# A transposed scratch image with x outermost, a residual moved in one transfer per step, and gathered pixels kept in channel order

## The chip, the cores and the metric

The kernel runs on one core of a Trainium2 chip. A core has TensorE (PE, matrix multiplies), VectorE (DVE), ScalarE (ACT), GpSimd (POOL) and SyncE (SP); each works through its own instructions in order, and they wait for one another by semaphores. Data lies in device memory (DRAM), in the on-chip memory of 128 partitions (SBUF) or in TensorE's output memory (PSUM). Transfers are done by 16 DMA engines, which all queues share; in this kernel nearly all DMAs are issued by GpSimd, a smaller part by SyncE. The metric is the device time of one execution in microseconds (us); lower is better.

## The reference

There are two layers over `x` of shape (8, 32, 128, 128), that is 8 images of 32 channels. `_gn` is a normalisation over groups of two channels. The first layer finds, for every pixel, the 8 of 25 neighbouring offsets with the smallest patch distance, gathers the 8 shifted pixels in each of the 32 channels, and works on the 256 gathered channels; channel `c*8 + k` holds channel `c` at the k-th best offset.

```python
def layer0(x, dct_w, w1, w2, w3, w4, w5, w6, inv_dct_w, agg_w):
    xb = patch_match_stack(x)              # (8, 256, 128, 128), channel c*8 + k
    dct = conv(xb, dct_w, groups=32)       # mixes the 8 pixels of one channel c
    h = relu(conv(conv(xb, w1), w2, groups=256, pad=1))   # 1x1, then 3x3 per channel
    h = relu(conv(conv(h, w3), w4, groups=256, pad=1))
    wiener = sigmoid(conv(conv(h, w5), w6, groups=256, pad=1))
    filt = conv(wiener * dct, inv_dct_w, groups=32)
    return conv(filt, agg_w)               # back to 32 channels

x = x + layer0(_gn(x), ...)
x = x + conv5x5(_gn(x), kernel)            # the same 5x5 kernel for each channel
```

## The kernel before

**Preparing an image.** `prep` loads an image with four groups of 32 rows over four groups of 32 partitions (`xn`, L81), normalises it (L384) and starts two things. `sources` (L399) makes a transposed copy for the gather: eight times, TensorE transposes four rows of each group into PSUM (L407), ScalarE copies the result to `xs` (L409), and GpSimd stores it, one DMA per row of the four, into the DRAM tile `xl` (L411). `xl` is laid out as (y, x, channel). Then 30 DMAs from DRAM to DRAM (L424), and two more for the borders (L429), spread it into `xtd`, in which the pixels that one gather tile needs lie together. `squares` and `costs` compute the patch distances: VectorE subtracts (L444), ScalarE squares (L452), TensorE sums over channels into `pd` (L459), ScalarE copies to `sm` (L470), GpSimd stores to `sq` (L474) and reads back into `dsum` (L492, L499); VectorE sums over the patch into `v` (L508 and on) and takes the 8 best of 25 (L536, L537). `places` turns them into bytes and stores them in the DRAM tile `idxd` (L573).

**Gathering.** A unit is four rows of half an image's width. `gather_load` brings the pixels `xt` (L591) and the indices `ib` (L602, one of three buffers, so it waits for the selection three units back). `gather_select` makes one-hot rows `sel` from `ib` on ScalarE (L616, L617). `gather_pixels` multiplies them with the pixels on TensorE (L631), copies the result to `xb` on ScalarE (L638) and, after every fourth unit, stores `xb`, eight rows of all 256 gathered channels, to the DRAM tile `xbd` with one DMA of 1 MB (L640). In `xb` partition `32 j + c` and index `g` hold channel `c` at offset `k = 2 j + g`; `xbd` has the same order, (128, 2, y, x).

**Filtering.** A step is eight rows. Each image has 17 steps, the last for the rows that the three 3x3 convolutions lag behind. For each of three stages the 1x1 convolution runs on TensorE (L670, L694) and the 3x3 one half on VectorE (L724) and half on TensorE (L750), which first needs rows moved between partitions, the transfers `t<-t` on SyncE's queue (L706, L708). `final_load` fetches the residual `xr` (L780, four DMAs, one per quarter of the partitions) and the gathered pixels `xf` (L790, eight DMAs, because the 256 channels must lie on the partitions in the order that `ldct` needs, while `xbd` keeps them by offset). `final_dct` applies `dct_w` on TensorE into `pc` (L809) and multiplies it in on VectorE (L817); `final_add` applies the aggregation into `pa` (L830), adds the residual (L838), takes statistics (L839) and stores the sum to the DRAM tile `x1d` (L843, four DMAs). The first and last step of an image have fewer than eight rows and use a layout of their own; the other 15 are `whole`. `layer1` reads `x1d` back (`xy`, `xm`), applies the 5x5 kernel on TensorE (L923) and stores to the output (L937).

**Order.** The order on TensorE, VectorE and ScalarE is written out by hand: the main loop runs over 17 x 8 steps (and two more to drain), in each over the stages 3, 2, 1 and 0 (0 is the final part), and works on one gather unit per stage. The preparation of the next image is cut into pieces that stand in queues, from which the loop takes VectorE work against a budget, and the rest as soon as it is due. GpSimd's instructions keep an order of their own, in which a DMA waits until its data and its buffer are ready and everything behind it waits too. `final_load` of a step is issued at the end of the loop's turn, one step ahead of its use. `mixes` (L300) builds `ldct` and the combined weights `lagg` once at the start, `weights` the others.

Of the kernel before, what the change touches and what calls it, by code (L numbers as in the profile page):

```python
# [8 lines left out]
F32 = mybir.dt.float32  # L9
# [7 lines left out]
P = 128  # L17
C, K, H, W = 32, 8, 128, 128
CK = C * K
NO = 25  # L20
R = 8
NS = H // R
TW = 11
# [13 lines left out]
C_M32 = C_G2 + 32  # L37
# [7 lines left out]
def bm3d_conv_preact(  # L45
# [16 lines left out]
    nc = tc.nc  # L62
# [237 lines left out]
    def mixes():  # L300

        dq = work.tile([P, 2, K], F32, name="dq", tag="dq", bufs=1)
        src = dct_w.rearrange("(m h c i) k a b -> m h k c (i a b)", m=2, h=2, i=K)
        for k in range(K):
            for m in range(2):
                for h in range(2):
                    p = 64 * h + 32 * (k % 2) + 8 * (k // 2)
                    nc.sync.dma_start(dq[p : p + 8, m], src[m, (h + m + 1) % 2, k])
        m8 = work.tile([P, 8], F32, name="m8", tag="m16", bufs=1)
        yield "D", 1.0, 10  # L310
        nc.vector.tensor_reduce(
            m8,
            cst[:, C_M32 : C_M32 + C].rearrange("p (a c) -> p c a", c=8),
            axis=mybir.AxisListType.X,
            op=ALU.add,
        )
# [82 lines left out]
    def sources(b, xn):  # L399


        xl = dram.tile([H, W, C], F32, name=f"xl_{b}", tag="xl")
        for r in range(0, 32, 4):
            yield "P", 0
            pt = ps_x.tile([P, 4, P], F32, name=f"px_{b}_{r}", tag="x")
            for q in range(4):
                nc.tensor.transpose(pt[:, q], xn[:, 3 + r + q, 2 : 2 + W], ident)  # L407
            xs = work.tile([P, 4, P], F32, name=f"xs_{b}_{r}", tag="ct")
            nc.scalar.copy(xs, pt)  # L409
            for q in range(4):  # L410
                nc.gpsimd.dma_start(  # L411
                    xl.rearrange("(g r) x c -> r x g c", g=4)[r + q],
                    xs[:, q].rearrange("p (g c) -> p g c", c=C),
                )
        xt = xtd[b] = dram.tile([H, QW, NT, C], F32, name=f"xtd_{b}", tag="xtd")
        for j in range(QW):
            for f in range(2):
                ta, tz = f * (NT // 2), (f + 1) * (NT // 2)
                if j < 2 and f == 0:
                    ta += 1  # L420
                if HW * f + TW * (NT // 2 - 1) + j - 2 >= W:
                    tz -= 1
                xa = HW * f + TW * (ta - f * (NT // 2)) + j - 2
                nc.gpsimd.dma_start(  # L424
                    xt[:, j, ta:tz], xl[:, xa : xa + TW * (tz - ta - 1) + 1 : TW]
                )
        jz = W + 2 - HW - TW * (NT // 2 - 1)
        for ja, jz, t, at in ((0, 2, 0, 0), (jz, QW, NT - 1, W - 1)):
            nc.gpsimd.dma_start(  # L429
                xt[:, ja:jz, t], xl[:, at : at + 1].to_broadcast([H, jz - ja, C])  # L430
            )

    def squares(b, i, pd, xn, aa, sq, idx):
# [186 lines left out]
    def gather_pixels(b, s4, f):  # L620
# [16 lines left out]
                )  # L637
        nc.scalar.copy(xb[:, :, 4 * h : 4 * h + 4, HW * f : HW * (f + 1)], pg)  # L638
        if h == 1 and f == 1:
            nc.gpsimd.dma_start(xbd[b][:, :, R * n : R * (n + 1)], xb)  # L640

# [88 lines left out]
    def depthwise_t(i, b, n):  # L732
# [33 lines left out]
        rows_before_t(i, b, n)  # L766
        accs[i, b, n][0] = acc

    def final_load(b, n):
        j0, j1 = (3, R) if n == 0 else (0, R if n < NS else 3)  # L770
        ya, yz = R * n - 3 + j0, R * n - 3 + j1

        whole = j1 - j0 == R
        nr, nw = (2, W) if whole else (j1 - j0, C)
        xr = work.tile([P, 2 * W], F32, name=f"xr_{b}_{n}", tag="xr")
        xr = xr[:, : nr * nw].rearrange("p (r w) -> p r w", w=nw)
        for j in range(4):
            ra = ya + 2 * j if whole else ya
            xa = 0 if whole else C * j
            nc.gpsimd.dma_start(  # L780
                xr[C * j : C * (j + 1)], x[b, :, ra : ra + nr, xa : xa + nw]
            )

        xf = xbp.tile([P, 2, R, W], F32, name=f"xf_{b}_{n}", tag="xf", bufs=1)
        src = xbd[b].rearrange("(j m h c) g y x -> g m h j c y x", j=4, m=2, h=2)
        for m in range(2):
            for h in range(2):
                for g in range(2):
                    p = 64 * h + C * g
                    nc.gpsimd.dma_start(  # L790
                        xf[p : p + C, m, j0:j1], src[g, m, (h + m + 1) % 2, :, :, ya:yz]
                    )
        return xr, xf, j0, j1

    def final_dct(b, n, acc, xf, j0, j1):
# [23 lines left out]
    def final_add(b, n, acc, xr, j0, j1):  # L819
# [17 lines left out]
        yield  # L837
        nc.vector.tensor_add(xr, xr, pa)  # L838
        nc.vector.bn_stats(stats[b][:, n], xr)  # L839
        for j in range(4):  # L840
            ra = ya + 2 * j if whole else ya
            xa = 0 if whole else C * j
            nc.gpsimd.dma_start(  # L843
                x1d[b][:, ra : ra + nr, xa : xa + nw], xr[C * j : C * (j + 1)]
            )

    def layer1(b):
# [186 lines left out]
    with tc.manual_schedule(engines=ORDERED):  # L1034
        push(prep(0))
        push(weights())
        push(mixes())
        xbd[0] = dram.tile([P, 2, H, W], F32, name="xbd_0", tag="xbd")
        for i in range(3):
            nc.gpsimd.memset(tb[i][0:64, :, 0], 0.0)  # L1040
        for u in range(7):
# [12 lines left out]
        for s in range(len(steps) + 2):  # L1054
            if s < len(steps):
# [5 lines left out]
                    push(prep(b + 1))  # L1061
                if n == NS - 1 and b + 1 < NB:
                    until(lambda: b + 1 in ready, 4.0)
                    xbd[b + 1] = dram.tile([P, 2, H, W], F32, name=f"xbd_{b+1}", tag="xbd")
            for i in (3, 2, 1, 0):
                si = s - (i - 1 if i else 2)
                live = 0 <= si < len(steps)
# [109 lines left out]
```

## Time and profile before

| What | Before |
|---|---|
| Median of 3 runs | 6640.18 us |
| Lowest and highest run | 6636.07 and 6641.82 us |
| The profiled execution: time, span | 6645.45 us, 6643.7 us |
| Mean granted clock of TensorE | 0.978 |
| Busy: PE, DVE, ACT, POOL | 6238.3, 5862.9, 5054.4, 3079.3 us |
| POOL instructions | 5015 |
| DMA | 770751 packets, 886.20 MB, mean 133 GB/s |

The span runs from the first to the last instruction. Busy time leaves out register, branch and semaphore instructions; on POOL a `DMA_DIRECT2D` row is the time that GpSimd takes to issue one transfer, not the transfer. "<-" after an idle time names what ended the wait; where several things are waited for, it is the one that came last by the profile's records, and it can be wrong. "The chain that ended last" is found by walking back from the last instruction, each time to what released it. Tiles are named without their numbers: `xf<-xbd` is a transfer from `xbd` to `xf`.

### The profile page before, as it was taken

The numbers are of one execution on the slowest core, as the hardware profiler recorded it, in microseconds if no ns is written. First come the engines' busy times: TensorE is split into PE (matmuls) and PEld (weight loads), VectorE is DVE, ScalarE is ACT, GpSimd is POOL, SyncE is SP. The second block draws the span as 40 slices with busy tenths as digits, with TensorE's granted clock in tenths as the row PEclk, the third lists the DMA queues.
The fourth block names the chain that finished last, engine by engine and source line by source line (L and its number), as shares of the span: only waits on it lengthen the run. The fifth ranks groups of instructions, "written<-read, shape, count | busy, mean of one in ns | idle before, by whom it ended". The sixth has DMA issues, their size and how long they took to land.

```text
span 6643.7 us, 234197 instructions
## 1 busy us (share of the span) xinstructions
PE 6238.3 (94%) x102306; PEld 3236.5 (49%) x102306; DVE 5862.9 (88%) x8828; ACT 5054.4 (76%) x6698; POOL 3079.3 (46%) x5015
## 2 busy tenths in 40 slices
PE   5898899999999999999999999999999999999997
PEld 1444455544555545544555544554445544454553
DVE  7889988999889998898989998899888999887786
ACT  5787778777787777877778877887769777687772
POOL 8354346444464343643446444464435543344334
PEclk8899999999999999999999999999999999999998
DMA  4555555656555564655646656465555655556553
GB/s 85 126 138 130 131 131 130 148 134 140 131 143 136 130 147 118 149 134 133 144 121 147 147 126 149 120 154 136 130 137 132 148 136 130 125 141 145 137 133 82
DMA packets 770751, 886.20 MB, mean 133 GB/s; under 512 B 248880, under 2 KB 614000, under 8 KB 769728
## 3 DMA queue, kind: packets, MB, share of 16 engines
q0 software_dynamic: 383648, 611.87, 36.9%
q1 hardware_dynamic: 383568, 258.11, 17.6%
q8 instruction: 805, 13.19, 0.9%
q10 hardware_dynamic: 2512, 1.25, 0.1%
q14 instruction: 218, 1.79, 0.1%
HBM read 420.60 MB, written 216.49 MB: 96 GB/s over the span
## 4 chain that ended last, share of the span: by engine, by line
PE 43%; DVE 29%; DMA 9%; ACT 8%; POOL 6%; issue 4%; SPq 0%; ACTq 0%; DVEq 0%; POOLq 0%
DVE acc L724 20%; PE pw L750 14%; PE pv L670 11%; PE p L694 9%; PE pg L631 3%; DMA t<-t 3%; POOL xtd L424 2%; DVE df L444 2%; DVE idx L537 2%; PE pc L809 2%; ACT sel L616 2%; ACT df L452 2%; DMA xf<-xbd 2%; DVE acc L817 1%; PE p L923 1%
## 5 line engine op out<-in xcount | busy, mean ns | idle before, releaser
L724 DVE SCALAR_TENSOR_TENSOR acc<-tv,dwv,acc 128x1024 f32<-128x1024 f32 (+3 forms) x3264 | 4032.3, 1237 | 240.8 <-ACT acc L721 136.8
L750 PE MATMUL pw<-t,dwd 96*32 96x254 f32 (+7 forms) x31680 | 2124.6, 420 | 51.0 <-DMA t<-t 38.4
L750 PEld LDWEIGHTS pw<-t,dwd 96*32 96x32 f32 (+1 forms) x31680 | 1088.4, 110 | 874.5 <-issue 411.2
L616 ACT ACTIVATE sel<-ib,nplace 128x1024 f32<-128x1024 uint8 x1024 | 1172.1, 1145 | 37.4 <-DMA ib<-idxd 37.4
L617 ACT ACTIVATE sel<-sel 128x1024 f32<-128x1024 f32 x1024 | 1085.7, 1060 | 32.5
L694 PE MATMUL p<-acc,lw 128*32 128x256 f32 x16768 | 1002.9, 383 | 24.7 <-ACT tv L678 23.3
L670 PE MATMUL pv<-acc,lw 128*32 128x512 f32 x8448 | 956.2, 590 | 48.7 <-DVE acc L817 43.4
L602 POOL DMA_DIRECT2D ib<-idxd x512 | 292.5, 571 | 1241.8 <-ACT sel L616 1176.2
L790 POOL DMA_DIRECT2D xf<-xbd x1088 | 651.9, 631 | 316.1 <-PE pc L809 180.1
L694 PEld LDWEIGHTS p<-acc,lw 128*32 128x32 f32 x16768 | 579.2, 111 | 437.1 <-issue 79.4
L452 ACT ACTIVATE df<-df 128x786 f32<-128x786 f32 (+2 forms) x576 | 468.6, 861 | 340.5 <-DVE df L444 337.8
L631 PE MATMUL pg<-sel,xt 120*32 120x88 f32 (+1 forms) x24576 | 616.1, 244 | 63.6 <-ACT sel L617 50.7
L631 PEld LDWEIGHTS pg<-sel,xt 120*32 120x32 f32 x24576 | 556.8, 110 | 235.0 <-ACT sel L617 70.1
L678 ACT COPY tv<-pv 128x512 f32<-128x512 f32 (+2 forms) x784 | 437.1, 579 | 305.0 <-PE pv L670 293.0
L444 DVE TENSOR_TENSOR df<-xn 128x786 f32<-128x786 f32 (+2 forms) x576 | 531.6, 973 | 81.2 <-PE pd L459 80.2
L728 ACT ACTIVATE acc<-acc 128x1024 f32<-128x1024 f32 (+3 forms) x408 | 417.3, 1023 | 241.6 <-DVE acc L724 241.3
L763 ACT ACTIVATE acc<-pw 128x512 f32<-128x512 f32 (+2 forms) x808 | 438.5, 573 | 182.7 <-PE pw L750 182.0
L670 PEld LDWEIGHTS pv<-acc,lw 128*32 128x32 f32 x8448 | 286.0, 111 | 534.1 <-issue 428.7
L701 ACT COPY t<-p 128x512 f32<-128x512 f32 x800 | 424.4, 571 | 118.0 <-PE p L694 118.0
L721 ACT ACTIVATE acc<-tv,dwv 128x1024 f32<-128x1024 f32 (+3 forms) x408 | 454.9, 1115 | 33.9 <-PE pa L830 20.6
L670 PE MATMUL pv<-xb,lw 128*32 128x512 f32 x4096 | 473.5, 596 | 0.0
L694 PE MATMUL p<-xb,lw 128*32 128x256 f32 x8192 | 468.5, 379 | 1.0 <-DVE xy L935 0.9
(155 smaller groups left out, 5932.9 us busy)
## 6 DMA issues: line engine op xcount, KB each, us to landing
ib<-idxd POOLq DMA_DIRECT2D x512, 256.0 KB, 4.1
xbd<-xb POOLq DMA_DIRECT2D x128, 1024.0 KB, 5.9
xf<-xbd POOLq DMA_DIRECT2D x960, 128.0 KB, 7.1
t<-t SPq DMA_DIRECT2D x792, 128.0 KB
t<-t SPq DMA_DIRECT2D x384, 256.0 KB
tv<-tv SPq DMA_DIRECT2D x384, 130.0 KB
xt<-xtd POOLq DMA_DIRECT2D x240, 180.0 KB, 3.7
xtd<-xl POOLq DMA_DIRECT2D x192, 96.0 KB, 3.5
```

The source lines that it names most:

```text
L444: nc.vector.tensor_sub(df[:, :, ca:cz], xn[:, r0 : r0 + SR, ca:cz], xn[:, r0 + dy : r0 + dy + SR, ca + dx : cz + dx],)
L452: nc.scalar.activation(df[:, :, ca:cz], df[:, :, ca:cz], AF.Square)
L616: nc.scalar.activation(sel, ib, AF.Square, bias=nplace)
L617: nc.scalar.activation(sel, sel, AF.Relu, scale=-1.0, bias=1.0)
L631: nc.tensor.matmul(pg[C * j : C * (j + 1), :, :, xa:xz], xt[: 8 * QW, f * (NT // 2) + t], sels[j // 2][: 8 * QW, j % 2 * 2 : j % 2 * 2 + 2 ...
L670: nc.tensor.matmul(ps[C * j : C * (j + 1), :hr], lhsT[:, g, P + C * j : P + C * (j + 1)], src(g)[:, h : h + hr], start=g == 0, stop=g == 1,)
L694: nc.tensor.matmul(ps[C * r : C * (r + 1), e, :nb], lhsT[:, g, s], rows[:, r : r + 4 * nb - 3 : 4], start=g == 0, stop=g == 1,)
L721: nc.scalar.activation(acc, rows, AF.Copy, scale=tap)
L724: nc.vector.scalar_tensor_tensor(acc, rows, tap, acc, op0=ALU.mult, op1=ALU.add)
L750: nc.tensor.matmul(pt[u][C * j : C * (j + 1), ka:kz, :nb, xa:xz], dwd[0:hi, i - 1, u, j, dx + 1], t[0:hi, j, ka:kz, :nb, xa + dx : xz + dx ...
L763: nc.scalar.activation(rows[:, u : u + 2 * nh[u] - 1 : 2, :nb], pt[u][:, : nh[u], :nb], funcs[i - 1])
L790: nc.gpsimd.dma_start(xf[p : p + C, m, j0:j1], src[g, m, (h + m + 1) % 2, :, :, ya:yz])
```

## The change

- `xl` becomes (x, y, channel). The copy to `xs` puts the four rows of a group next to each other, so that a piece of four rows by 32 channels (512 B) is contiguous on both sides, and one DMA replaces four. The reads into `xtd` take the same pixels with the new strides.
- `xbd` becomes (256, y, x) in the reference's channel order `c*8 + k`. Its store takes four DMAs, one per `j`, in place of one.
- `xf` is read in whole blocks of channels with three DMAs in place of eight. The halves of the first block are still swapped.
- The residual's load and the store of its sum take one DMA in place of four in the 15 whole steps.
- `mixes` lays the weights out to suit: the rows of `dq` go to partition `64 h + 8 c + k` in place of `64 h + 32 (k % 2) + 8 (k / 2) + c`, with the same number of loads, and the mask `m8` is taken from other columns of the constants.

```diff
@@ mixes
-        src = dct_w.rearrange("(m h c i) k a b -> m h k c (i a b)", m=2, h=2, i=K)
-        for k in range(K):
+        src = dct_w.rearrange("(m h c i) k a b -> m h c k (i a b)", m=2, h=2, i=K)
+        for c in range(8):
             for m in range(2):
                 for h in range(2):
-                    p = 64 * h + 32 * (k % 2) + 8 * (k // 2)
-                    nc.sync.dma_start(dq[p : p + 8, m], src[m, (h + m + 1) % 2, k])
+                    p = 64 * h + K * c
+                    nc.sync.dma_start(dq[p : p + K, m], src[m, (h + m + 1) % 2, c])
...
-            cst[:, C_M32 : C_M32 + C].rearrange("p (a c) -> p c a", c=8),
+            cst[:, C_M16 : C_M16 + 16].rearrange("p (a c) -> p c a", c=8),
@@ sources
-        xl = dram.tile([H, W, C], F32, name=f"xl_{b}", tag="xl")
+        xl = dram.tile([W, H, C], F32, name=f"xl_{b}", tag="xl")
...
-            nc.scalar.copy(xs, pt)
-            for q in range(4):
-                nc.gpsimd.dma_start(
-                    xl.rearrange("(g r) x c -> r x g c", g=4)[r + q],
-                    xs[:, q].rearrange("p (g c) -> p g c", c=C),
-                )
+            nc.scalar.copy(
+                xs.rearrange("p g (q c) -> p q g c", c=C),
+                pt.rearrange("p q (g c) -> p q g c", c=C),
+            )
+            nc.gpsimd.dma_start(
+                xl.rearrange("x (g r) c -> x g (r c)", g=4)[:, :, C * r : C * (r + 4)], xs
+            )
...
                 nc.gpsimd.dma_start(
-                    xt[:, j, ta:tz], xl[:, xa : xa + TW * (tz - ta - 1) + 1 : TW]
+                    xt[:, j, ta:tz],
+                    xl[xa : xa + TW * (tz - ta - 1) + 1 : TW].rearrange("x y c -> y x c"),
                 )
@@ gather_pixels
-            nc.gpsimd.dma_start(xbd[b][:, :, R * n : R * (n + 1)], xb)
+            for j in range(4):
+                nc.gpsimd.dma_start(
+                    xbd[b].rearrange("(c j g) y x -> j c g y x", j=4, g=2)[
+                        j, :, :, R * n : R * (n + 1)
+                    ],
+                    xb[C * j : C * (j + 1)],
+                )
@@ final_load (by_rows is image[:, ya : ya + R] as "c (j r) w -> j c (r w)")
-        for j in range(4):
-            ra = ya + 2 * j if whole else ya
-            xa = 0 if whole else C * j
+        if whole:
+            nc.gpsimd.dma_start(by_channel(xr), by_rows(x[b], ya))
+        for j in range(0 if whole else 4):
             nc.gpsimd.dma_start(
-                xr[C * j : C * (j + 1)], x[b, :, ra : ra + nr, xa : xa + nw]
+                xr[C * j : C * (j + 1)], x[b, :, ya : ya + nr, C * j : C * (j + 1)]
             )
...
-        src = xbd[b].rearrange("(j m h c) g y x -> g m h j c y x", j=4, m=2, h=2)
-        for m in range(2):
-            for h in range(2):
-                for g in range(2):
-                    p = 64 * h + C * g
-                    nc.gpsimd.dma_start(
-                        xf[p : p + C, m, j0:j1], src[g, m, (h + m + 1) % 2, :, :, ya:yz]
-                    )
+        for m, to, at, size in ((0, 0, 64, 64), (0, 64, 0, 64), (1, 0, P, P)):
+            nc.gpsimd.dma_start(xf[to : to + size, m, j0:j1], xbd[b][at : at + size, ya:yz])
@@ final_add
-        for j in range(4):
-            ra = ya + 2 * j if whole else ya
-            xa = 0 if whole else C * j
+        if whole:
+            nc.gpsimd.dma_start(by_rows(x1d[b], ya), by_channel(xr))
+        for j in range(0 if whole else 4):
             nc.gpsimd.dma_start(
-                x1d[b][:, ra : ra + nr, xa : xa + nw], xr[C * j : C * (j + 1)]
+                x1d[b][:, ya : ya + nr, C * j : C * (j + 1)], xr[C * j : C * (j + 1)]
             )
```

More of the change, by code (lines that the diff above doesn't have):

```diff
@@ L429, in sources @@
             nc.gpsimd.dma_start(
-                xt[:, ja:jz, t], xl[:, at : at + 1].to_broadcast([H, jz - ja, C])
+                xt[:, ja:jz, t], xl[at].unsqueeze(1).to_broadcast([H, jz - ja, C])
             )
@@ L767, in depthwise_t, with by_channel, by_rows @@
         accs[i, b, n][0] = acc
+    def by_channel(xr):
+        return xr.rearrange("p r w -> p (r w)")
+    def by_rows(image, ya):
+        return image[:, ya : ya + R].rearrange("c (j r) w -> j c (r w)", j=4)
     def final_load(b, n):
@@ L1037, in bm3d_conv_preact @@
         push(mixes())
-        xbd[0] = dram.tile([P, 2, H, W], F32, name="xbd_0", tag="xbd")
+        xbd[0] = dram.tile([CK, H, W], F32, name="xbd_0", tag="xbd")
         for i in range(3):
@@ L1063, in bm3d_conv_preact @@
                     until(lambda: b + 1 in ready, 4.0)
-                    xbd[b + 1] = dram.tile([P, 2, H, W], F32, name=f"xbd_{b+1}", tag="xbd")
+                    xbd[b + 1] = dram.tile([CK, H, W], F32, name=f"xbd_{b+1}", tag="xbd")
             for i in (3, 2, 1, 0):
```

## The prediction

> **What bounds the kernel now.** I read the page first (busy shares, then the chain of work that ended last), then the waits, the groups of GpSimd (POOL), the DMA issues, and last the timelines of the two places where the chain runs over POOL.
>
> ```profile
> PE 6238.3 (94%) x102306; PEld 3236.5 (49%) x102306; DVE 5862.9 (88%) x8828; ACT 5054.4 (76%) x6698; POOL 3079.3 (46%) x5015
> PE 43%; DVE 29%; DMA 9%; ACT 8%; POOL 6%; issue 4%; SPq 0%; ACTq 0%; DVEq 0%; POOLq 0%
> ```
>
> TensorE is busy for 6238.3 of 6643.7 us, so all its idle time is 405 us. The first 250 us hold about 113 of it and the last 94 us another 43, by the busy times of those stretches; some 250 us are left for the eight images. The change edits only DMAs (nearly all issued by POOL) and one ScalarE copy, so it can win only where one of these 405 us hangs on POOL or a transfer. The waits, named engine first, with total us, number and longest:
>
> ```profile
> PE pg L631 <- ACT sel L617: 50.7, 33, 2.3
> PE pw L750 <- DMA t<-t: 38.4, 27, 4.0
> ACT sel L616 <- DMA ib<-idxd: 37.4, 7, 6.9
> POOL ib L602 <- ACT sel L616: 1176.2, 248, 14.4
> POOL xr L780 <- DMA x1d<-xr: 70.1, 36, 4.2
> ```
>
> No row has TensorE waiting for `xf`, `xbd`, `xr` or `x1d`, the transfers that the change regroups in every step. The third row is the lead: seven times, once per image prepared after the first, ScalarE stands still for an index load, and right after it, in six of the seven, TensorE waits 2.2 us for the selection (first row; 1.8 for another tile in the first). The second row is a transfer on SyncE's queue, which shares the 16 DMA engines with everything here.
>
> **What POOL's issues cost.** Busy us and mean ns of one, then idle before it:
>
> ```profile
> L790 POOL DMA_DIRECT2D xf<-xbd x1088 | 651.9, 631 | 316.1 <-PE pc L809 180.1 <-DMA out_dram<-xy 83.3 <-DMA xf<-xbd 21.5
> L843 POOL DMA_DIRECT2D x1d<-xr x544 | 277.3, 517 | 313.5 <-DVE xr L838 259.7 <-DMA xf<-xbd 26.5 <-DMA xbd<-xb 7.9
> L780 POOL DMA_DIRECT2D xr<-in_x_dram x544 | 276.9, 515 | 140.0 <-DMA x1d<-xr 70.1 <-DVE acc L724 56.1 <-DVE df L444 4.6
> L424 POOL DMA_DIRECT2D xtd<-xl x240 | 197.0, 833 | 6.2 <-DMA xl<-xs 4.7 <-DMA xbd<-xb 1.3
> L411 POOL DMA_DIRECT2D xl<-xs x256 | 193.9, 764 | 128.3 <-ACT xs L409 92.0 <-ACT tmp_b L265 20.0 <-issue 11.7
> L640 POOL DMA_DIRECT2D xbd<-xb x128 | 90.9, 710 | 206.3 <-ACT xb L638 200.9 <-issue 2.1 <-PE pv L670 1.2
> ```
>
> An issue costs 0.5 to 0.83 us and depends little on size, so POOL's time goes with the count. `xl` falls from 256 to 64 issues, `xf` from 1088 to 408; `xr` and `x1d` each from 544 to 184 (15 of the 17 steps of an image are whole and go from 4 to 1); `xbd` rises from 128 to 512. At the old cost each, with 0.6 for a quarter of `xbd`: -147 - 387 - 185 - 186 + 216 = -689 us, which takes POOL from 3079 to about 2390 us. None of it counts by itself: POOL idles for half the span.
>
> **Place one, the start: -5 us.** POOL is on the path here:
>
> ```profile
> 65.78 3.04 POOL L411 DMA_DIRECT2D xl<-xs  x4
> 68.81 0.69 POOL L492 DMA_DIRECT2D dsum<-sq  x1
> 69.49 7.10 POOL L499 DMA_DIRECT2D dsum<-sq  x12
> 79.03 1.11 DVE L508 TENSOR_TENSOR v<-dsum 128x910 f32<-128x910 f32 x1 [6.06 <-DMA xl<-xs]
> ```
>
> POOL runs without a gap from 47 us on, and VectorE waits 6.06 us (the releaser's name is off: `v` needs `dsum`, whose last issue ends at 76.6, 2.45 earlier). With one issue in place of four per `xl` group POOL is no longer behind: the second block's `sq` store can go when its ScalarE copy ends (59.9 in place of 63.6), takes 2.2 to issue and 1.9 to land (64.0), then 7.8 us of `dsum` issues and 2.45 to land: 74.3 in place of 79.0, and VectorE is free at 73.0. That is -4.7; the chain stays with VectorE, which is nearly gapless up to the first pixels. Bounds: 0 to -6.06.
>
> **Place two, seven times, the burst of `xtd`: -15 us.** The image prepared around 2740 us:
>
> ```profile
> 2739.25 0.67 POOL L640 DMA_DIRECT2D xbd<-xb  x1 [1.25 <-ACT xb L638]
> 2740.06 24.63 POOL L424 DMA_DIRECT2D xtd<-xl  x30
> 2764.68 1.48 POOL L429 DMA_DIRECT2D xtd<-xl  x2
> 2766.16 4.62 POOL L790 DMA_DIRECT2D xf<-xbd  x8
> 2773.24 0.59 POOL L474 DMA_DIRECT2D sq<-sm  x1 [2.46 <-ACT tv L678]
> 2774.43 1.66 POOL L474 DMA_DIRECT2D sq<-sm  x3 [0.61 <-DMA xf<-xbd]
> 2776.83 0.59 POOL L602 DMA_DIRECT2D ib<-idxd  x1 [0.74 <-DMA xf<-xbd]
> ```
>
> POOL is in order, so `ib` stands behind 26 us of `xtd` issues and eight `xf` issues; it lands too late and ScalarE idles 5.91 us at 2780.6. The waits of 2.46, 0.61 and 0.74 us fit a limit of eight transfers in flight: each ends as the `xf` eight issues back lands (2766.2 + 7.1 = 2773.2). After the change: `xbd` +1.9 (four issues of 0.6 and not one; it is gated by ScalarE's copy, so the shorter `xl` group ahead of it buys nothing here), `xf` -2.7 (three of 0.65 and not eight), the three waits -3.8, since eight back is then an `xtd`, long landed. Together `ib` comes 4.6 us earlier, 5 to 6 where the `xl` group is not gated, against stalls of 5.0 to 6.9 (2.0 at the first). So most of it goes, and with it TensorE's wait: 6 x 2.2 + 1.8 = -15. Bounds: 0, if VectorE (90 to 96% busy in these stretches) sets the pace; -37, if all of ScalarE's wait counts. I take TensorE's row, because VectorE itself waits for TensorE soon after (`xr` for `pa`, about 3 us).
>
> **Behind the output stores: -2 us.** Once per image the chain goes from `out_dram` (11 us to land) over `xf`, `x1d` and `xr` to `v`, transfers that wait for one eight issues back. VectorE's own wait there is 2.5 us in 4 places; with fewer issues in flight it goes. Bounds 0 and -6.
>
> **The rest: 0, with cover named.** The regrouped transfers:
>
> ```profile
> ib<-idxd POOLq DMA_DIRECT2D x512, 256.0 KB, 4.1
> xbd<-xb POOLq DMA_DIRECT2D x128, 1024.0 KB, 5.9
> xf<-xbd POOLq DMA_DIRECT2D x960, 128.0 KB, 7.1
> x1d<-xr POOLq DMA_DIRECT2D x480, 32.0 KB, 3.2
> ```
>
> An `xf` of 128 KB lands later than an `ib` of twice the size: its source, four groups of eight channels, is the likely cause. The new `xf` has plain rows like `xbd`, so I take about 6 us for the whole megabyte, not 5 of issuing and 7.1. It is asked for one step (48 us) ahead, which hides either. The new `xr` and `x1d` have a source or target in four groups, as the old `xf` had: 7.1 us to land in place of 3.2, but 1.5 us less issuing. Behind the later landing POOL's `xr` load waits up to 2.4 us longer, with `xf` and `ib` behind it; these are two units (24 us) ahead of use, so 0. If that cover were gone in the 36 steps where it waits already: +86. Residual traffic is not read sooner than a step later.
>
> The Trainium skill ("DMA: Bandwidth & Descriptors", section "Why a DMA increments its semaphore by 16 and not by 1") says that a transfer uses the largest number of engines, at most 16, that divides the slowest dimension of both sides: 4 for the old `xf` and the new residual, 16 for the new `xf`. That speaks against the one-transfer residual; by it the sum would still be the same, since only POOL waits for that landing.
>
> The `xs` copy writes in permuted order: ScalarE's strided copy `acc<-pw` takes 573 ns and the contiguous `t<-p` 571, so 0 (twice the time would be 4.6 us of an idle-enough engine per image). The setup loads of `dq` keep their number (32 on SyncE's queue) and piece size: 0. `xtd` reads pieces of the same size in another order, with 30 issues 0.82 apart: up to 6.6 us of landing (now 3.5) no issue waits, so 0; the `xl` stores get longer pieces, bounds 2.5 us to land as now and 4.9, the row of `xy<-x1d`, hidden either way except once before the burst (+2.4 x 7 = +17 at worst).
>
> **The sum.** -5 - 15 - 2 = -22 on the profiled execution's 6645.45 us (span 6643.7), which is 5.3 above the median 6640.18 of the runs: about 6618 from the median, -0.33%. What this kernel's measurement tells from no change is about 0.2%, 13 us.
>
> **Rivals.** (1) VectorE sets the pace in the images and only the start counts: 6640 - 5 = 6635, within 0.2%. For: 88% busy, and up to 96% there. Against: the chain leaves the burst over `ib`, `sel` and `pg`, not VectorE. Chance 0.2. (2) The reordered reads of `xl` land slowly. From 6.6 us of landing on, the eight in flight hold POOL back; at 10 us an issue comes every 1.25 us, 13 more per burst: the start +13, and after the -5; seven stalls are 8 longer, of which TensorE sees about half, +28: 6640 - 5 + 13 + 28 = 6676. For: x is now 16 KB apart. Against: along y pieces are now neighbours. Chance 0.08. The Trainium skill (same page, "Latency and other measured facts") reports that bandwidth halves from a row pitch of 512 KiB to one of 4 MiB; were that so here, far below its range, the landing would be 7 us, an estimate, and a burst 30 x (7/8 - 0.82) = 1.6 us longer; no row of this trace shows it. (3) The megabyte of `xf`, now in one burst on SyncE's `t` transfers, makes TensorE wait more in row `PE pw <- DMA t<-t`. At that row's mean (1.4 us) in every fourth of 136 steps: +48, 6666; it decides from 0.26 us a step on. For: that row exists wherever `out_dram` fills the engines. Against: `xbd` is already such a burst and is split in four now. Chance 0.12. (4) All of the 5.3 us stalls and other POOL waits count: 6640 - 5 - 37 - 6 = 6592. Chance 0.15. The forecast itself: 0.45.
>
> Faster by over 0.2%: the forecast, (4) and a shade of (1): 0.62. Within: the rest of (1): 0.18. Slower: (2) and (3): 0.20. The range reaches from below (4), 6584, to past (1) and half of (3), 6656; the forecast's own is 6600 to 6627.
>
> **What would show it.** POOL near 2400 us with some 3800 instructions; no `ACT sel <- DMA ib` row, or a few us; `v` at 74 us in the start; `xf` landing near 6 us, `x1d` near 7. A `t<-t` row well over 38, or `xtd` landing over 6.6 us, would make me wrong; so would a missing `ib` row with TensorE's idle time unchanged.

## The result: 0.65% slower, and the profile after

The changed kernel takes 6685.09 us (median of 4 runs, 6679.93 to 6692.59) against 6641.0 us (4 runs, 6636.07 to 6652.68) of the kernel before on the same chip: a ratio of 1.0065, 95% interval 1.0049 to 1.0081. It is slower by about 44 us; 22 us faster was forecast. The profiled execution of after took 6692.59 us, with a span of 6690.8 us (before 6643.7) and a mean granted clock of TensorE of 0.973 (before 0.978).

First the page of after: busy time of each engine, and the shares of the chain of work that ended last.

```profile
PE 6254.4 (93%) x102306; PEld 3218.8 (48%) x102306; DVE 5863.1 (88%) x8828; ACT 5056.3 (76%) x6698; POOL 2392.8 (36%) x3807
PE 51%; DVE 25%; ACT 8%; DMA 8%; issue 5%; POOL 3%; SPq 0%; ACTq 0%; POOLq 0%; DVEq 0%
```

GpSimd does what was forecast to the instruction: 2392.8 us and 3807 instructions. It helped nothing in sum: its share of the chain fell from 6% to 3%, and PE's rose from 43% to 51%. Now the waits of after (total us, number, longest), engine that waits first:

```profile
PE pw L758 <- DMA t<-t: 73.5, 30, 7.0
PE pw L758 <- issue: 45.2, 19, 5.8
PE pg L633 <- ACT sel L619: 37.8, 27, 2.4
ACT sel L618 <- DMA ib<-idxd: 11.1, 6, 2.5
POOL ib L604 <- ACT sel L618: 1461.9, 276, 21.4
POOL xr L792 <- DMA x1d<-xr: 43.2, 17, 8.0
```

Two rows fell as forecast: ScalarE's wait for `ib` from 37.4 to 11.1 us, and PE's wait for `sel` from 50.7 to 37.8. Two rose: PE's wait for the halo, the rows that `t<-t` moves between partitions, from 38.4 to 73.5 us, and a row "issue" of the same matmuls from 5.4 to 45.2. In before that row is:

```profile
PE pw L750 <- issue: 5.4, 5, 2.0
```

The second row is for the most part the same wait under another name: in 13 of its 19 cases in after, 33 of the 45 us, PE starts 0.1 us after a `t<-t` has landed, and the profile books "issue" (one case is shown further down). What the other six waited for it doesn't tell. Both rows together went from 43.8 to 118.7 us, 75 more.

The transfers of after (KB each, median us from issue to landing):

```profile
xbd<-xb POOLq DMA_DIRECT2D x512, 256.0 KB, 5.1
xf<-xbd POOLq DMA_DIRECT2D x240, 256.0 KB, 4.5
xf<-xbd POOLq DMA_DIRECT2D x120, 512.0 KB, 7.7
xtd<-xl POOLq DMA_DIRECT2D x192, 96.0 KB, 3.3
x1d<-xr POOLq DMA_DIRECT2D x120, 128.0 KB, 4.3
xr<-in_x_dram POOLq DMA_DIRECT2D x120, 128.0 KB, 5.2
```

None of the regrouped transfers is slow in itself. What they do to their neighbours is the subject of the rest.

**Where PE falls behind.** TensorE's 102306 matmuls stand in the same order in both kernels, but for some 370 that changed places with a neighbouring group, so the start of each can be compared with that of the same one before. At 300 us PE is 4 us ahead. Then, over the seven images that prepare or finish beside another one, two places of each are worth a look. In the 37 us that hold one of the groups of output stores (`out_dram`), PE falls behind by 37.4 us in sum. In the 74 us that hold the burst of `xtd` and its tail, the sum is 4.4, but it hides two large ones: counted from each burst's own first issue, PE gains 25.5 us between 40 and 77 us behind it (3.3 to 6 at each of the last six bursts, nothing at the first), and loses 24.9 in the 37 us after that. All the rest is 3.9, and 5.3 at the end: 47.0.

Here is the output place of the third image. GpSimd of before, a timeline (start us, us, line, what, number of issues; idle before and what ended it):

```profile
2086.45 0.71 POOL L640 DMA_DIRECT2D xbd<-xb  x1 [10.19 <-ACT xb L638]
2091.43 6.09 POOL L937 DMA_DIRECT2D out_dram<-xy  x4 [4.28 <-DVE df L444]
2097.52 2.33 POOL L790 DMA_DIRECT2D xf<-xbd  x4
2101.59 0.57 POOL L790 DMA_DIRECT2D xf<-xbd  x1 [1.74 <-DMA out_dram<-xy]
2103.83 0.57 POOL L790 DMA_DIRECT2D xf<-xbd  x1 [1.68 <-DMA out_dram<-xy]
2106.57 0.57 POOL L790 DMA_DIRECT2D xf<-xbd  x1 [2.17 <-DMA out_dram<-xy]
```

And GpSimd of after at the same place:

```profile
2080.42 0.56 POOL L643 DMA_DIRECT2D xbd<-xb  x1 [11.26 <-ACT df L454]
2083.01 6.04 POOL L945 DMA_DIRECT2D out_dram<-xy  x4 [2.03 <-DVE xy L943]
2089.04 1.62 POOL L643 DMA_DIRECT2D xbd<-xb  x3
2090.65 0.54 POOL L800 DMA_DIRECT2D xf<-xbd  x1
2092.43 0.52 POOL L800 DMA_DIRECT2D xf<-xbd  x1 [1.24 <-DMA out_dram<-xy]
2094.21 0.56 POOL L800 DMA_DIRECT2D xf<-xbd  x1 [1.26 <-DMA out_dram<-xy]
2096.78 0.55 POOL L604 DMA_DIRECT2D ib<-idxd  x1 [2.02 <-DMA out_dram<-xy]
```

In both, GpSimd stands still from the ninth transfer on until an output store, the one eight issues back, has landed: eight may be in flight, whatever their size. Before, the ninth and the following were `xf` of 128 KB; when the halo's `t<-t` was issued (2099.76) 4 stores of 124 and 4 `xf` of 128 KB, 1008 KB, were under way. After, three quarters of the gathered store have come behind the output stores, and `xf` is in pieces of 256 and 512 KB: at 2092.65 there were 3 x 124 + 3 x 256 + 2 x 256 = 1652 KB, and in the next 10 us another 512 KB of `xf`, an `ib`, an `x1d`, an `xy` and an `xm` came in. The two `t<-t` landed after 10.4 and 10.7 us before, and after 13.4 and 15.2 us now (from the issue to the last rise of its semaphore). TensorE of before goes through the 96 matmuls that use them without a wait:

```profile
2108.34 5.65 PE L750 MATMUL pw<-t,dwd 96*32 96x256 f32 x96
```

TensorE of after:

```profile
2102.25 2.79 PE L758 MATMUL pw<-t,dwd 96*32 96x256 f32 x48
2108.56 4.05 PE L758 MATMUL pw<-t,dwd 96*32 96x256 f32 x36 [3.52 <-issue]
```

The second `t<-t`, issued at 2093.29, landed at 2108.47, and PE goes on at 2108.56. This is not one bad case. All 381 `t<-t` of 256 KB after the first 250 us, by the KB that GpSimd had in flight when they were issued:

| KB in flight | before: number, mean us to land | after: number, mean us to land |
|---|---|---|
| none | 89, 3.5 | 90, 3.4 |
| to 300 | 151, 4.3 | 119, 4.0 |
| 300 to 600 | 64, 4.9 | 76, 5.3 |
| 600 to 900 | 34, 5.9 | 34, 6.7 |
| 900 to 1200 | 29, 7.2 | 22, 6.7 |
| 1200 to 1500 | 5, 9.1 | 12, 8.5 |
| over 1500 | 9, 7.5 | 28, 11.3 |

Up to 1500 KB the relation is much the same in both; after has three times as many cases above that, and they take longer there (11.3 us against 7.5).

### The profile page after: what moved, and what is told of

The parts are those of the page before. It is cut to its first block, busy times and chain, and to the rows that moved or that the text cites. A ratio compares the mean times of both kernels' runs of the same rounds, so it can differ in the third digit from the quotient of the medians.

```text
span 6690.8 us, 232449 instructions
## 1 busy us (share of the span) xinstructions
PE 6254.4 (93%) x102306; PEld 3218.8 (48%) x102306; DVE 5863.1 (88%) x8828; ACT 5056.3 (76%) x6698; POOL 2392.8 (36%) x3807
## 4 chain that ended last, share of the span: by engine, by line
PE 51%; DVE 25%; ACT 8%; DMA 8%; issue 5%; POOL 3%; SPq 0%; ACTq 0%; POOLq 0%; DVEq 0%
PE pw L758 17%; DVE acc L732 16%; PE pv L678 13%; PE p L702 11%; DMA t<-t 4%; PE pg L633 4%; DVE idx L539 2%; PE pc L817 2%; DVE df L446 2%; ACT df L454 2%; ACT sel L618 2%; PE p L931 2%; POOL xtd L425 1%; DVE acc L825 1%; PE pa L838 1%
## 5 line engine op out<-in xcount | busy, mean ns | idle before, releaser
L758 PE MATMUL pw<-t,dwd 96*32 96x254 f32 (+7 forms) x31680 | 2157.1, 424 | 122.3 <-DMA t<-t 73.5
L618 ACT ACTIVATE sel<-ib,nplace 128x1024 f32<-128x1024 uint8 x1024 | 1172.4, 1145 | 11.1 <-DMA ib<-idxd 11.1
L633 PE MATMUL pg<-sel,xt 120*32 120x88 f32 (+1 forms) x24576 | 612.3, 243 | 46.3 <-ACT sel L619 37.8
L729 ACT ACTIVATE acc<-tv,dwv 128x1024 f32<-128x1024 f32 (+3 forms) x408 | 455.0, 1115 | 34.6 <-PE pa L838 20.2
L640 ACT COPY xb<-pg 128x512 f32<-128x512 f32 x512 | 301.7, 589 | 150.2 <-PE pg L633 145.5
```

The source lines that it names most:

```text
L618: nc.scalar.activation(sel, ib, AF.Square, bias=nplace)
L633: nc.tensor.matmul(pg[C * j : C * (j + 1), :, :, xa:xz], xt[: 8 * QW, f * (NT // 2) + t], sels[j // 2][: 8 * QW, j % 2 * 2 : j % 2 * 2 + 2 ...
L729: nc.scalar.activation(acc, rows, AF.Copy, scale=tap)
L758: nc.tensor.matmul(pt[u][C * j : C * (j + 1), ka:kz, :nb, xa:xz], dwd[0:hi, i - 1, u, j, dx + 1], t[0:hi, j, ka:kz, :nb, xa + dx : xz + dx ...
```

## The experiments

All "before" times below are of the kernel before on the same chip in the same series. A table at the end of this section puts the places side by side.

**One part at a time.** The three parts of the change alone, and the change without the residual's part. The edits are those of the diff above, cut to one part; for the last:

```diff
@@ after, final_load and final_add as before
-        if whole:
-            nc.gpsimd.dma_start(by_channel(xr), by_rows(x[b], ya))
-        for j in range(0 if whole else 4):
+        for j in range(4):
```

> The kernel before with the transposed image x outermost alone. Theory A (the loss is a pile-up: with fewer and larger transfers the limit of eight in flight lets megabytes of xbd, xf and index loads queue at once, and the t transfers of SyncE wait behind them): this part takes 24 issues per image off GpSimd and adds no bytes in flight, so the start is 5 to 6 us shorter and about 6625 to 6637 us come out, with the row of TensorE waiting for t<-t near 38 us as before. Theory B (the one-transfer residual, with a target in four groups, clogs some of the DMA engines): the same as A here. Theory C (the reordered reads of xl are slow): xtd<-xl lands well later than 3.5 us and the time is over 6655 us.

> The kernel before with the gathered pixels in channel order alone (xbd stored by four DMAs, xf read by three, mixes to suit). Theory A: most of the loss is here, 6665 to 6690 us, the wait of TensorE for t<-t with what is put down to issue 80 us and more in place of 43. Theory B: no loss, 6625 to 6645 us, t<-t near 38. Theory C: no loss.

> The kernel before with the residual's load and the store of its sum in one transfer each per whole step. Theory A: 360 issues less for each, no more bytes in flight than 128 KB each: 6635 to 6650 us. Theory B: the loss is here, 6670 to 6690 us, with more t transfers over 10 us while x1d<-xr is in flight. Theory C: no loss.

> The kernel after with the residual's load and store put back to four DMAs each, the other parts kept. Theory A: near the kernel after, 6665 to 6690 us, perhaps a little less because eight more issues in flight again hold GpSimd back. Theory B: 6615 to 6640 us, the gains of the other parts without the loss. Theory C: near the kernel after.

Measured, beside 6642.56 us: only the image with x outermost 6632.02 us, ratio 0.998 (0.9971 to 0.9989), faster; only the channel order 6721.17 us, 1.0115 (1.01 to 1.0129), 79 us slower; only the residual 6644.19 us, 1.0003 (0.9994 to 1.0013), no change; all but the residual 6682.09 us, 1.0058 (1.0045 to 1.0071), as after. So the loss is in the channel-order part; alone, neither the residual's four groups (its 128 KB land in 4.4 us) nor the reads of `xl` cost time. Theory A had named the part and not the size: it asked for 6665 to 6690 us. The parts don't add: the channel order costs 79 us alone and 50 on top of x outermost. The waits of the kernel with the channel order alone:

```profile
PE pw L756 <- DMA t<-t: 80.1, 30, 6.8
PE pw L756 <- issue: 45.4, 16, 8.0
ACT sel L616 <- DMA ib<-idxd: 32.3, 7, 7.2
```

**Store or reads?** The channel order splits the store of `xbd` in four and merges the reads of `xf` from eight to three. GpSimd's order pulls the four apart: in 13 of 128 stores of after other transfers go between them (12 times the four output stores, once the burst of 32 `xtd`). One run splits the store in the old layout, one reads `xf` in eight pieces in the new one, one lets ScalarE issue the four stores; a fourth joins the two harmless parts.

```diff
@@ xbd4: before
-            nc.gpsimd.dma_start(xbd[b][:, :, R * n : R * (n + 1)], xb)
+            for j in range(4):
+                s = slice(C * j, C * (j + 1))
+                nc.gpsimd.dma_start(xbd[b][s, :, R * n : R * (n + 1)], xb[s])
@@ after_xf8: after
-            nc.gpsimd.dma_start(xf[to : to + size, m, j0:j1], xbd[b][at : at + size, ya:yz])
+            for q in range(0, size, C):
+                nc.gpsimd.dma_start(
+                    xf[to + q : to + q + C, m, j0:j1], xbd[b][at + q : at + q + C, ya:yz]
+                )
@@ after_act: after, the four stores
-                nc.gpsimd.dma_start(
+                nc.scalar.dma_start(
```

> The kernel before with its one gathered store per step cut into four transfers of 32 partitions, in the old layout; everything else is as before, the eight 128-KB reads of xf too. Two parts of the channel-order edit can make the halo copies t<-t late. Theory A1: it is the four issues of the store, which GpSimd's order pulls apart (other transfers go between them) and which then land behind them. It expects +25 to +80 us, with the wait of PE pw for the halo's transfer clearly over the 38 us of before, at 55 or more. Theory A2: it is the reads of xf, which put a megabyte in flight in three issues where eight issues let it in piece by piece. It expects nothing of this kernel: within 15 us of before, the wait at 30 to 45 us.

> The kernel after with each step's xf read in eight transfers of 32 partitions (128 KB each) in place of three of 256, 256 and 512 KB; the layout, the four stores and all else are as after. Theory A2 (the merged reads) expects most of the loss back: 6625 to 6645 us, and the wait of PE pw for the halo near 40 us. Theory A1 (the torn store) expects the loss to stay: 6670 us or more, the wait still over 60 us. More POOL time is certain, 600 issues of some 0.55 us, about 330 us, beside an engine that idles over 60% of the span.

> The kernel after with the four stores of the gathered pixels issued by ScalarE, right behind the copy that fills them, in place of GpSimd; nothing can come between them there, and the limit on GpSimd's transfers doesn't hold them. ScalarE pays 512 issues, some 0.05 to 0.6 us each, 25 to 300 us of its 1580 us of idle time. Theory A1 expects the torn stores gone and 6630 to 6650 us, with the halo's wait at 45 us or less, unless ScalarE's issues themselves are dear: then PE waits for ACT instead. Theory A2 expects the halo's wait to stay at 60 us or more, and the time at 6670 us or more.

> The kernel before with the first two parts of the change alone: the image transposed with x outermost, and the residual in one transfer each way; the gathered pixels stay in their old order. Both theories (A1 and A2) put the whole loss into the third part, so both expect the sum of the two measured parts, 10.5 less and 1.7 more: 6625 to 6638 us, faster than before. If the parts act on one another, as the third did with the first (79 us more alone, some 40 more with the others), it could lie some 10 us to either side.

Measured, beside 6643.64 us: the split store 6704.8 us, 1.0091 (1.0074 to 1.0108); after with eight reads 6681.08 us, 1.0056 (1.0039 to 1.0073); ScalarE's stores 6728.72 us, 1.0132 (1.0115 to 1.0149); the two harmless parts 6642.35 us, 0.9999 (0.9989 to 1.0009). By the total times A1 held for the split store and for the eight reads, and A2 fell; A1's figures for the halo's row did not come (46.9 us where 55 or more was asked, 52.0 where over 60). By the places it is not so either. With eight reads PE's loss at the output stores fell from 37.4 to 9.2 us, as A2 said, and as much was lost anew at the `xtd` bursts, 31.7 in place of 4.4. The waits of after with eight reads:

```profile
PE pw L758 <- DMA t<-t: 52.0, 31, 5.0
PE pc L820 <- DVE acc L828: 38.3, 8, 6.7
ACT sel L618 <- DMA ib<-idxd: 37.8, 7, 7.4
```

ScalarE again waits 38 us for `ib`, which stands behind the burst and now behind eight `xf` issues too. The row of `pc` (0.8 us in after) lies at the bursts as well: at one of them, in the run with a split store and a priority (below), ScalarE stands still for `ib` for 12.5 us, and PE at `pc` for 6.0. It isn't `xf` that PE waits for there: in after with eight reads the last `xf` had landed some 7 us before each such wait of 5 us and more began, and with the split store in the old layout 1 us and more before. The split store in the old layout, which has eight reads too, shows the same two rows, and larger:

```profile
PE pc L811 <- DVE acc L819: 56.9, 9, 12.5
ACT sel L616 <- DMA ib<-idxd: 57.5, 7, 9.9
```

So with eight reads the split store loses some 30 us at the bursts in either layout, and the merged reads of after had paid for it. ScalarE as the issuer took nearly all of the loss at the output stores away (4.6 us are left), but PE lost 80 us all over the images. The profile puts part of ScalarE's idle time down to the store:

```profile
L454 ACT ACTIVATE df<-df 128x786 f32<-128x786 f32 (+2 forms) x576 | 466.3, 861 | 407.9 <-DVE df L446 251.8 <-DMA xbd<-xb 115.8 <-issue 16.2
```

Most of that is ScalarE's own issuing, which isn't counted as busy: its 512 issues take 399 us in all (25 to 300 had been expected), and 112 of the 137 us of idle time that the profile puts down to `xbd` are spent on them. That price hides what the run was to tell. The time is the one that A2 asked for, the `t<-t` row of 48.0 us fits neither theory, and A1 had made dear issues its exception. The two harmless parts together lost the 10 us that one of them gains, where 6625 to 6638 us had been expected; the `t<-t` row is 52.8 us there, 35.7 with x outermost alone. Why is open; in the last column of the table below, which holds the tail of the bursts, they lose 28.2 us, and x outermost alone 19.8.

**The store held together.** A priority in GpSimd's scheduler puts the four issues of a store ahead of whatever else is ready; then none of the 128 stores is pulled apart. On after, on the split store in the old layout, and, as a control, on before.

```diff
+            with tc.high_priority():
-            for j in range(4):
+                for j in range(4):
...
```

> The kernel after with the four issues of each gathered store put ahead of whatever else is ready in GpSimd's order (a high priority in the scheduler), so that nothing goes between them in any of the 128 stores; layout, number and size of the transfers are as after. In the trace of after 13 stores are pulled apart: one by a burst of 32 xtd transfers and twelve by four output stores each. Comparing matmul by matmul, PE falls behind the kernel before by 37 us over seven images in the 37 us that hold the output stores, and by 16 us in those of the xtd burst. Theory A1 (the torn store): most of this comes back, 6625 to 6650 us, and the wait of PE pw for the halo falls to 30 to 50 us. Theory A3 (four transfers instead of one crowd the queue wherever they stand, torn or not): the loss stays, 6670 us or more.

> The kernel before with its gathered store cut in four of 32 partitions, as in the run of that alone (61 us slower), and now with the same priority, so that the four stay together. Theory A1: 6635 to 6655 us, near before, and the 57 us that PE waited at the final product pc (its xf late) nearly gone. Theory A3: 6690 us or more, as without the priority.

> The kernel before with its one gathered store under the same priority, a control: what the priority does by itself to a store that can't be torn. Theories A1 and A3 both expect little, within 10 us of before (6633 to 6653 us). If it were 20 us faster or slower, the priority would act by other ways than keeping the four together, and the two other runs would have to be read against this one.

Measured, beside 6647.25 us: after 6664.99 us, 1.0026 (1.0013 to 1.0039); the split store 6702.31 us, 1.0085 (1.0061 to 1.011); before 6670.19 us, 1.0041 (1.0027 to 1.0056). The control's expectation missed: the priority alone costs 0.41%. It changes the order around the bursts, where ScalarE then waits 60.4 us for `ib` (37.4 without). On after, 0.39 of the 0.65% came back, some 25 us, short of what A1 asked for (6625 to 6650 us, and the halo's row at 30 to 50, where it is 62.0), though no store is torn any more; PE's loss at the output stores is still 28.6 us. So the torn store is the smaller part there, some 9 us by this count. In the old layout with eight reads it is all there is at the output stores (16.1 to 0.4 us), and the loss at the burst stays (35.7), with ScalarE's wait for `ib` at 81.8 us and the row of `pc` at 49.8; so A1's 6635 to 6655 us and a `pc` row nearly gone, the latter put down to a late `xf`, both missed.

**The reads, place by place.** By then the merged reads were suspected to cost at the output stores and to pay at the bursts. The output stores of an image fall in steps 3 to 7 of the next. One run reads `xf` in eight pieces in these steps and in three elsewhere, one the other way round, and the third adds the priority to the first.

```diff
@@ after_mix: after, final_load
-            nc.gpsimd.dma_start(xf[to : to + size, m, j0:j1], xbd[b][at : at + size, ya:yz])
+            part = C if 3 <= n <= 7 else size
+            for q in range(0, size, part):
+                nc.gpsimd.dma_start(
+                    xf[to + q : to + q + part, m, j0:j1],
+                    xbd[b][at + q : at + q + part, ya:yz],
+                )
@@ after_anti
+            part = C if not 3 <= n <= 7 else size
```

> The kernel after with xf read in eight transfers of 128 KB in steps 3 to 7 of every image, in which the output stores of the image before go out, and in three elsewhere. Theory A2' (the merged reads cost beside the output stores, because GpSimd has eight transfers in flight whatever their size, and elsewhere they help ib to be on time): 6640 to 6660 us, the halo's wait of PE pw at 40 to 55 us, and ACT's wait for ib still at 5 to 15 us. Theory A3 (the four stores are the cost, wherever the reads stand): 6675 us or more, as after and after_xf8.

> The reverse of after_mix: eight reads of xf in all steps but 3 to 7, three reads in those, where the output stores are. Theory A2' expects both losses together: 6695 to 6720 us, the halo's wait at 60 us or more, and ACT's wait for ib at 30 to 45 us. Theory A3 expects it where after and after_xf8 are, 6675 to 6690 us.

> after_mix with the priority that keeps the four stores of a step together. The priority took 20 us off after; if the two remedies add, 6620 to 6645 us, at or below the kernel before (theory A2' with a share of tearing). Theory A3: 6660 us or more, as after_pri. The priority by itself made the kernel before some 27 us slower, by later ib; if that shows here too, ACT's wait for ib is over 30 us and the time is near 6665 us.

Measured, beside 6643.71 us: 6645.25 us, 0.9999 (0.9989 to 1.0009); the other way round 6716.96 us, 1.0109 (1.0092 to 1.0127); with the priority 6634.77 us, 0.9981 (0.997 to 0.9991). Two kernels with the same edit in different steps are 72 us apart, on either side of after. The waits of the first, then of its reverse:

```profile
PE pw L758 <- DMA t<-t: 56.6, 33, 7.0
ACT sel L618 <- DMA ib<-idxd: 13.0, 6, 3.6
```

```profile
PE pw L758 <- DMA t<-t: 46.7, 29, 4.1
PE pc L822 <- DVE acc L830: 41.1, 8, 7.8
PE pw L758 <- issue: 38.1, 14, 6.3
ACT sel L618 <- DMA ib<-idxd: 37.4, 7, 7.6
```

Two figures missed: the first one's `t<-t` row was to be 40 to 55 us and is 56.6, and the reverse's was to be 60 or more; it is 46.7, and 84.8 with its "issue" row. The priority, a loss on before, is a gain here, since ScalarE's wait for `ib` is only 4.8 us. This kernel, with eight reads in steps 3 to 7 and the priority, is 0.19% faster than before, about as much as x outermost alone.

PE's start of the same matmul against before, in us (profiled executions), by place: the first 380 us; seven times the 37 us with output stores; seven times the 74 us of the burst; the rest; and the sum. The last two columns go across these places: they count each of the seven bursts from its own first issue in before, from 40 to 77 us and from 77 to 114 us behind it:

| Kernel | Start | Output stores | `xtd` bursts | Rest | Sum | Burst, 40 to 77 | Burst, 77 to 114 |
|---|---|---|---|---|---|---|---|
| after | -4.0 | +37.4 | +4.4 | +9.2 | +47.0 | -25.5 | +24.9 |
| only x outermost | -6.8 | -1.6 | -10.2 | +8.5 | -10.2 | -20.2 | +19.8 |
| only channel order | +3.6 | +35.6 | +31.4 | +8.6 | +79.3 | +30.5 | +8.4 |
| all but the residual | +1.2 | +35.9 | -10.5 | +2.6 | +29.3 | -20.8 | +7.3 |
| split store, old layout | +1.2 | +16.1 | +30.3 | +13.9 | +61.6 | +35.5 | +6.7 |
| after, eight reads | -5.1 | +9.2 | +31.7 | +8.8 | +44.5 | +30.1 | +10.3 |
| after, priority | -3.9 | +28.6 | +2.8 | +2.9 | +30.4 | -25.5 | +27.4 |
| after, eight reads in steps 3 to 7 | -4.1 | +9.6 | -5.5 | +0.3 | +0.3 | -24.9 | +21.3 |
| the reverse | -6.3 | +34.3 | +32.8 | +13.3 | +74.0 | +32.1 | +6.3 |
| eight reads in 3 to 7, priority | -5.8 | +0.3 | -3.6 | +0.6 | -8.5 | -26.4 | +27.1 |

Each row is one execution. Most sums agree with the differences of the medians to 3 us; those of all but the residual (39.5 by the medians), of eight reads (37.4) and of the priority (17.7) are 7 to 13 us off. A difference of some 10 us between two cells is not sure by itself.

And how many `t<-t` that feed `pw` took over 10 us: 38 before, 67 in after, 66 in the reverse, 44 with eight reads in steps 3 to 7, and 28 with the priority on top.

The column of the output stores splits: some 28 us go with the merged reads (37.4 to 9.2, 37.4 to 9.6, 28.6 to 0.3), some 9 with the torn store (37.4 to 28.6, 9.6 to 0.3). Counted over the 37 us from the first issue of each group of stores, the shares are 30 to 39 and 10 to 16. That the merged reads are the larger part there holds in every pair.

The bursts don't split so. In the column "40 to 77" the kernels form two groups. Where ScalarE waits less for `ib` than before (4.8 to 22.5 us in place of 37.4), PE gains 20 to 26 us, and in each of these kernels it loses 7 to 27 in the 37 us after. The others lose 30 to 36, and a later `ib` is not the reason in all of them: with eight reads (37.8) and in the reverse (37.4) ScalarE waits as long as before.

What PE waits for at this place in those two is `pc`, 37.3 and 40.2 us; the second half of its matmuls goes on when VectorE's product of the first half (`acc` from `pc`) is done, while before all 16 run without that wait. In the channel order alone it is the halo, 30.2 us in both its rows, and none before. A store torn by the burst of `xtd` is not the reason either. It happens seven times in each kernel that loses 30 to 36 here, and once in after and in its kernel with eight reads in steps 3 to 7, so the pair of opposite runs differs in that too; but all but the residual tears seven and gains 20.8, and the split store with the priority tears none and loses 41.5.

That the number of reads matters at the bursts too is shown by the opposite runs, which are 57 us apart in this column; by which link, and what makes the channel order alone lose there when the same with x outermost gains, is open. Open too is whether the megabyte of `xf` itself delays the halo at the output stores, or the transfers which three free places let in behind it: no run kept one and took the other.

## Why the prediction was wrong

**What held.** *Place one, the start*: -5 forecast, and PE is 4 us ahead at 300 us (7 at 200 us). *Place two, its mechanism*: `ib` earlier, ScalarE's wait of 37.4 down to 11.1 us, and PE's row `pg <- sel` 12.9 us less against the 15 forecast; PE gains 25.5 us between 40 and 77 us behind the bursts' first issues, inside the bounds of 0 and 37. *POOL's issues*: 2392.8 us and 3807 instructions against 2390 and 3800 (the term of 387 goes by 0.65 us for each of the 408 `xf` issues left, and not by the old cost as the sentence says, which would make it 429). *The reads of `xl`*: 3.3 us of landing against 3.5 before, so rival (2) fell. *The residual*: no time; its landing was 4.3 us in place of the 7.1 taken from the old `xf`, so four groups on one side were not what made that slow. The Trainium skill ("DMA: Bandwidth & Descriptors", section "Why a DMA increments its semaphore by 16 and not by 1") gives both transfers four engines; the rows have 7.1 and 4.3 us for 128 KB, so the divisor alone does not tell the landing.

**What failed.** "The rest: 0, with cover named." Its claim for `xf`, that about 6 us for the megabyte asked for one step ahead "hides either", is right for `xf`: no row has PE waiting for it, though it was not 6 us: the last of the three lands 11.3 us (median) after the first issue (12.9 for the eight of before). The step counted the cover of the moved transfer and not the cover of those beside it. `t<-t` has no step of cover: where PE waits for one, it was issued 5 to 11 us ahead of that (9.5 in the median, before). And the prediction took the limit of eight in flight as a stall of GpSimd's that goes, which it is at the burst. At the output stores the same limit held the bytes in flight near 1 MB (1008 KB at the place shown), and with larger transfers it let in 1652. Where the step said 0, the halo's two rows grew by 75 us, against gains of 22 in the sum.

**The rival that came near.** Rival (3) named the row, the cause and the sign. Its price of 48 us, put on every fourth step, was too small for rows that grew by 75, and with the forecast's gains taken off it made 6666 us, where 6685 was measured. The loss is not spread: 20 stretches of 8 us, three per image, hold each over 2.2 us, 125 us together, against some 57 us of gains of the same size elsewhere. What was said against it, that the store "is split in four now", was a cost of its own: 61 us in the old layout. The chance of 0.12 was too low, it seems, because the rival was weighed by the size of one burst, and not by what is in flight at the one place where the output stores already land in 11 us.

**Given back later.** The 25.5 us won at the bursts went in the 37 us after, where +24.9 stand: at 1997 us, for one, the halo's copies are issued with an `xr`, two `xm` and an `ib` still under way, take 7.3 and 7.4 us in place of 3.5 and 3.3, and PE waits 2.8 us. So place two was worth more than was forecast, and nothing in sum: the stall removed ahead of the queue of transfers came back, for the larger part as a wait for the halo (26.2 us in these 37, 11.3 before). x outermost alone gives its gain back too, -20.2 and +19.8, there most of it in a wait for VectorE's `xy` (11.4 us).

## What to carry to other kernels

Where a queue allows a number of transfers in flight, as eight here, merging transfers raises the bytes in flight, and the price can fall on other queues' small, late-asked transfers: count KB under way when the latency-critical one is issued, not the issues saved. Judge a merge or split place by place, against what else is under way there; the same merge cost some 28 us at one place and saved some 27 at another. The choice by step brought the kernel back to the time of before (0.9999), and with the priority a little below it (0.9981). A transfer cut in several can be pulled apart by its queue's order, so look at the order of issues first.

## What was not expected of the hardware

A wait of PE costs more than itself. The span grew by 47.1 us, of which PE's idle time is 31.0 and its busy time 16.1, for the same 102306 matmuls. The stretches around the gap shown above, in after (window; us; busy us and number on PE, PEld, DVE, ACT and POOL; granted clock; share of the DMA engines; GB/s):

```profile
2102.00:2108.00 6.00, 3.04 (x75) 1.96 (x64) 5.86 (x6) 4.08 (x5) 2.51 (x4) 1.00 1.06 258
2108.00:2114.00 6.00, 5.44 (x52) 2.96 (x56) 5.82 (x6) 0.66 (x2) 1.84 (x3) 0.51 1.08 218
2114.00:2120.00 6.00, 6.00 (x68) 2.29 (x64) 1.30 (x2) 3.11 (x5) 0.00 (x0) 0.92 0.61 128
```

After 3.52 us of waiting the clock is granted at 0.51 for 6 us: the 48 matmuls behind the wait take 5.3 us, where before 96 of them took 5.65, and a loss of 3.5 becomes one of some 7. Of the gaps from 3.5 to 4.5 us, 7 of 7 (before) and 10 of 11 (after) have half clock in them or in the 9 us behind them, 5.4 and 5.8 us of it in the mean; of those from 0.4 to 2 us 17 of 96 and 19 of 82. Between 250 and 6550 us the clock is at half for 147 us before, 212 in after, 229 in the reverse and 164 in the fastest. The stretches are 3.4 us long, or twice and three times that. The Trainium skill ("TensorE: Matmul & The Clock Gate", section "Part 1: The HAM clock gate (the "warmup" mystery)") states that an idle window of about 3.4 us halves the clock until a busy one has passed; these lengths agree, but shorter gaps were followed by it too: 9 of 29 of 2 to 2.5 us before, and 9 of 30 in after, 8 of these 9 with no other gap of 0.1 us or more within 9 us. A sum of waits should carry this for those of 3.5 us and more: at half clock for 5.4 to 5.8 us, about 2.8 us come on top of a gap of 4, a factor of about 1.7 by these figures; the prediction had none.
